# Row maxima of masked attention scores by another VectorE instruction, with the requests for the shifts and the value products placed elsewhere

## The chip, the cores and the metric

The kernel runs on one core of a Trainium2 chip. The metric is device time in microseconds of one execution; a median over several executions is compared. The engines are TensorE (PE; its weight loads are shown as PEld), VectorE (DVE), ScalarE (ACT), GpSimd (POOL) and SyncE (SP, which here issues DMAs).

## What is computed

One layer: the rows of x (8 batches of 512 rows, 128 wide) are normalised, and the result goes through causal attention with 16 heads of 8 dimensions and through a mixture of 8 experts with top-2 routing beside one shared expert. Everything is added to x.

```python
def attn(x, W1, b1, Wp, bp):              # B, S, E = 8, 512, 128; H = 16 heads, d = 8
    h = x @ W1 + b1                       # q, k, v for each head
    w = einsum('bhqd,bhkd->bhqk', q, k) / sqrt(d)
    w = softmax(w * mask - (1.0 - mask) * 1e6, axis=-1)   # mask: lower triangle
    a = einsum('bhqk,bhkd->bhqd', w, v)
    return a @ Wp + bp

def ffn(x):                               # 4096 rows; hidden width 352
    shared = (silu(x @ gate.T) * (x @ up.T)) @ down.T
    probs = softmax(x @ gate_w.T); topw, topi = top_k(probs, 2)
    routed = sum over the two chosen experts of topw / sum(topw) * expert(x)
    return shared + routed

xn = layernorm(x)
out = x + attn(xn) + ffn(xn)
```

Everything is float32.

## The kernel before

**Groups, tiles and steps.** Attention goes by groups: a group n is four heads of one batch, so there are 8 x 4 = 32 groups. A group takes NTILES = 5 steps, one for each entry of TILES: two "wide" tiles, two "mixed" and one "half". Each holds 2 x 512 columns of scores for 128 keys a block. 32 x 5 = 160 steps make the main loop.

**What a step issues.** The order is written out by hand for PE, DVE, ACT and SP. A step does, in program order: on an odd group at i == 1 `fetch` (q and k of a later unit, on SP's queue); `weigh`, which computes transposed scores in PSUM (`fill`, tile scT, L339) and their exponential on ScalarE (pT, L465), with the triangle cut either by extra products (L324) or afterwards by POOL (L472); the pending writes of expert results (`to_place`); `look` for the tile nine steps ahead (AHEAD); `extra`, one piece of the expert layer (`chunk`: products gu, L651, tanh on ScalarE, L656, and two VectorE operations, L657 and L659), which also issues `load_weights` (L602, SP's queue, 576 KB an expert) and `load_slots` on POOL; one slice of the routing, until it is done; `side`, which runs what has fallen due and the down products (y, L682); and the value products that are waiting (`late`).

**Why row maxima are needed.** The exponential must have its row maximum subtracted. In the transposed scores a row's maximum would lie along partitions, so the maximum is worked out beforehand from scores that aren't transposed (`look`, `maxima`, `peak_scores`: products sc, L383) and put into q as two additional rows (a high and a low part) against rows of ones in k. `shift_parts` makes the two parts on VectorE at the group's last tile, `shift` turns them on TensorE (mT_ps, L439) and copies them (mT, L443) a step later, and `put_shift` sends them with two DMAs from SP into rows of qs (L449) a step after that. scT of the group then reads these rows.

**Row maxima before.** tops and diag hold maxima of 2 x 2 x 4 blocks of rows. For i = 0 and 2 (MASKED_TILES) the tile holds only the diagonal blocks, eight products of 128 columns. The mask comes in one of two ways: while the routing runs, by four products with the mask (mask_half, L324); afterwards `prepare` has ScalarE write the mask into the PSUM tile a step ahead (L371), and the products add to it. One reduction over 1024 columns gives diag (L417). For i = 1 and 3 the blocks in front of the diagonal of rows 3 and 1 are computed (384 and 128 columns for each of two heads) and reduced (L421, L422); for i = 4 those of row 2 for four heads (256 columns each; L412). tops starts at -3e38; row_max is the larger of tops and diag (L427).

**PSUM and SBUF.** The sc tile has one buffer of two banks (m_ps), scT one of two banks (w_ps), the value sums one bank (av_ps), and three banks (mi_ps) go round for all else, gu and y among them. pT comes from a pool of four buffers (pr).

**Value products.** `attend` multiplies pT with v_ext (av, L489), four heads side by side in four columns of the array. It is called twice in a group: behind step 1 for the two wide tiles (it runs in step 2), and behind step 4 for the mixed and half ones (it runs in step 0 of the next group).

**When the routing is over**, `some_routing` closes the pools that it used and opens those of the routed experts (later_pools).

Of the kernel before, what the change touches and what calls it, by code (L numbers as in the profile page):

```python
# [67 lines left out]
def attn_moe_kernel(  # L68
# [72 lines left out]
    def constant_rows(t, rows):  # L141
# [4 lines left out]
                fills[:rows].unsqueeze(1).to_broadcast([rows, NU * HP * NC, P]),  # L146
            )

    mask_q = const.tile([P, P], BF16, name="mask_q")
    nc.gpsimd.memset(mask_q, 0.0)  # L150
    nc.gpsimd.affine_select(
        out=mask_q, in_=mask_q, pattern=[[-1, P]], compare_op=ALU.is_ge, fill=MASKED,
        base=0, channel_multiplier=1,
    )
    eye_2 = const.tile([P, 2, P], BF16, name="eye_2")
    mask_q2 = const.tile([P, 2, P], BF16, name="mask_q2")
    mask_k2 = const.tile([P, 2, P], BF16, name="mask_k2")
    for m, sign, compare, fill in (
        (mask_q2, 1, ALU.is_ge, MASKED), (mask_k2, -1, ALU.is_ge, MASKED),
        (eye_2, 1, ALU.not_equal, 1.0),  # L160
    ):
# [29 lines left out]


    tops = const.tile([P, 2, 2, NC], F32, name="tops")
    nc.vector.memset(tops, LEAST)
    diag = const.tile([P, 2, 2, NC], F32, name="diag")

    xnT = const.tile([E, NT * P], F32, name="xnT")

# [162 lines left out]

    MASKED_TILES = (0, 2)
    ahead = []

    def prepare(n, i):

        ps = m_ps.tile([P, 2, S], F32, name="sc")
        if i in MASKED_TILES:  # L370
            nc.scalar.copy(  # L371
                ps.rearrange("p t (b k) -> p (t b) k", k=P),
                mask_q.unsqueeze(1).to_broadcast([P, 2 * NC, P]),
            )
        ahead.append(ps)

    def peak_scores(n, i):
        ready_ = bool(ahead)
        ps = ahead.pop() if ready_ else m_ps.tile([P, 2, S], F32, name="sc")

        def part(at_, jj, c, key, count, start):
            q, k = rows_of(n, jj, QK + 1 if n else QK)
            nc.tensor.matmul(  # L383
                ps[:, jj % 2, ts(at_, P) if count == 1 else ds(at_ * P, count * P)],
                lhsT=q[:, ts(c, P)], rhs=k[:, key * P : (key + count) * P],
                start=start, stop=True, skip_group_check=True,
            )

        j = i // 2 * 2
        if i == 4:  # L390
            blocks = [(0, 0, 2, 0, 2, True), (2, 2, 2, 0, 2, False)]
        elif i in MASKED_TILES:
            blocks = [(c, j, c, c, 1, not ready_ and c == 0) for c in range(NC)]
        else:
            blocks = [(0, j, 3, 0, 3, True), (3, j, 1, 0, 1, False)]
        for at_, jj, *rest in blocks:
            for t in range(2):
                part(at_, jj + t, *rest)
        if i in MASKED_TILES and not ready_:
            for k in range(2):  # L400
                for t in range(2):
                    mask_half(
                        ps[:, t].rearrange("p (b k) -> p b k", k=P), t, k,
                        mask_q2[ts(t, SIDE), k].unsqueeze(1).to_broadcast([SIDE, NC, P]),
                    )
        return ps

    def maxima(n, i):

        ps = peak_scores(n, i)  # L410
        if i == 4:
            nc.vector.tensor_reduce(  # L412
                tops[:, :, :, 2],
                ps.rearrange("p t (u k) -> p t u k", u=2), AX.X, ALU.max,
            )
        elif i in MASKED_TILES:
            nc.vector.tensor_reduce(  # L417
                diag[:, :, i // 2, :], ps.rearrange("p t (b k) -> p t b k", k=P), AX.X, ALU.max
            )
        else:  # L420
            nc.vector.tensor_reduce(tops[:, :, i // 2, 3], ps[:, :, : 3 * P], AX.X, ALU.max)  # L421
            nc.vector.tensor_reduce(tops[:, :, i // 2, 1], ps[:, :, 3 * P :], AX.X, ALU.max)  # L422

    def shift_parts(n):

        top = at.tile([P, 2, 2 * NC], F32, name="row_max")
        nc.vector.tensor_tensor(  # L427
            top.rearrange("p t (i c) -> p t i c", c=NC), tops, diag, ALU.max
        )
        parts = at.tile([P, 2, 2, 2 * NC], F32R, name="m_parts")  # L430
        hi, lo = parts[:, :, 0], parts[:, :, 1]
        nc.vector.tensor_scalar_mul(hi, top, -1.0)
        nc.vector.scalar_tensor_tensor(lo, top, -1.0, hi.bitcast(F32), ALU.mult, ALU.subtract)
        return parts

    def shift(n, parts):

        ps = misc([32, P], "mT_ps")
        nc.tensor.transpose(  # L439
            ps, parts.rearrange("p t r m -> p (t r m)").bitcast(F32), ident  # L440
        )
        mT = at.tile([32, P], F32R, name="mT")
        nc.vector.tensor_copy(mT, ps)  # L443
        return partial(put_shift, n, mT)

    def put_shift(n, mT):
        for t in range(2):
# [5 lines left out]
                mT[ts(t, 16)].bitcast(F32),  # L453
            )

    masked = []

    def on_pool():
        return tc.issue_after(masked[-1]) if masked else nullcontext()
# [1 line left out]
    def weigh(n, kind, j, by_pool, spare):  # L461

        ps = fill(n, kind, j, by_pool, spare)
        pT = pr.tile([P, 2, S], F32, name="pT")
        nc.scalar.activation(pT, ps, AF.Exp, scale=D**-0.5)  # L465
        if by_pool:
            if kind == "half":
                diagonals = [pT.rearrange("p t (u k) -> p (t u) k", u=2)[:, :, :P]]
            else:
                diagonals = [pT[:, :, :P]] + ([pT[:, :, 3 * P :]] if kind == "mixed" else [])  # L470
            for d in diagonals:
                m = nc.gpsimd.affine_select(  # L472
                    out=d, in_=d, pattern=[[0, d.shape[1]], [1, P]], compare_op=ALU.is_ge,
                    fill=0.0, base=0, channel_multiplier=-1,
                )
                masked.append(m.ins)
        return pT

    def attend(n, tiles, av):

        b, g = divmod(n, NG)

        def add(jj, c, weights):
            at_ = HH * (g % 2) + 4 * (g // 2) + jj
            nc.tensor.matmul(  # L489
                av[32 * jj : 32 * jj + 32, c * P :], lhsT=v_ext[b % NV][:, c, at_, :],  # L490
                rhs=weights, start=(c == 0 and g % 2 == 0), stop=(c == NC - 1 and g % 2 == 1),
                skip_group_check=True,
            )

        heads = [(j + t, pT[:, t]) for _, j, pT in reversed(tiles) for t in range(2)]
        if len(tiles) > 2:
            attend(n, tiles[:-1], av)
            attend(n, tiles[-1:], av)
            return
        kind = tiles[0][0]  # L500
        if kind == "wide":
            for jj, w in heads:
                add(jj, 0, w)
        elif kind == "mixed":
            for jj, w in heads:
                add(jj, 1, w[:, : 3 * P])
            for jj, w in heads:
                add(jj, 3, w[:, 3 * P :])
        else:
            for t, w in heads:  # L510
                for u in range(2):
                    add(2 * u + t, 2, w[:, ts(u, 2 * P)])
# [74 lines left out]
    stream += [("routed", j) for j in range(NB // MB)]  # L587
    stream += [("shared", j) for j in shared[FIRST:]]
    weights, held, turned, scales = {}, {}, {}, {}
    later_pools = {}  # L590

    def load_weights(k, c):

# [559 lines left out]
    def some_routing():  # L1153
        if not done_routing and next(routing, "end") == "end":
# [3 lines left out]
            later_pools["inp"] = pool("inp", 6)  # L1158
            later_pools["turned"] = pool("turned", 3)
            later_pools["scales"] = pool("scales", 4)  # L1160

    measure(0, NC)
    scale(0, 1)
# [45 lines left out]
    routed = -2  # L1209
    alone = set(range(3, 21, 2)) | {12, 16, 20}  # L1210
    for t in range(AHEAD):
        parts_then = look(t)
        extra()
        parts_then()
        if t - AHEAD >= routed:
            some_routing()
        side(t - AHEAD, 2)
        behind(t - AHEAD)
    for n in range(B * NG):
        b, g = divmod(n, NG)  # L1220
        waiting = []
        for i, (kind, j) in enumerate(TILES):
            step = n * NTILES + i
            if i == 1 and n % 2 == 1 and (n + 3) // 2 < 2 * B:
# [3 lines left out]
            waiting.append((kind, j, weigh(n, kind, j, by_pool, spare)))  # L1228
            while to_place:
                to_place.pop(0)()  # L1230
            parts_then = look(step + AHEAD) if step + AHEAD < total_steps else lambda: None
            if step not in alone:
                extra()
            parts_then()
            if done_routing and step + AHEAD + 1 < total_steps:
                prepare(*divmod(step + AHEAD + 1, NTILES))
            if step >= routed:
                some_routing()
            side(step, 2)
# [5 lines left out]
                evacuate(n, av, halves[0])  # L1245
            if i == 1 and g % 2 == 0:
                av = av_ps.tile([P, S], F32, name="av")
            if i in (1, 4) or (i == 3 and n == B * NG - 1):
                late = [partial(attend, n, waiting, av)]
                waiting = []  # L1250
            if len(placed) == NB:
# [89 lines left out]
```

## Time and profile before

| | |
|---|---|
| median of 3 executions | 564.23 us (562.38 to 564.98) |
| the profiled execution | 565.0 us, of which the span from first to last instruction is 562.8 us |
| granted TensorE clock, mean | 0.992 |

| group of instructions | count | mean of one |
|---|---|---|
| L383 sc, 128 / 256 / 384 columns | 620 / 124 / 124 | 259 / 296 / 380 ns |
| L417 diag, 1024 columns | 64 | 1221 ns |
| L421, L422, L412 tops, 768 / 256 / 1024 columns | 64 / 64 / 32 | 950 / 412 / 1220 ns |
| L371 ScalarE writes the mask | 50 | 1020 ns |
| L324 products with the mask into sc | 56 | 382 ns |
| L465 exponential | 156 | 1025 ns |
| L657, L659 VectorE for gu | 156, 156 | 416, 423 ns |
| L427 row_max | 32 | 166 ns |
| L602 expert weights, 576 KB | 40 | |
| L449 shifts into qs, 8 KB | 64 | |

A line of groups names line, engine, operation, tiles and shapes, count, then busy time and mean of one, then idle time before it and what ended that. A line of the timeline gives start, length, engine, line, operation and, in brackets, the idle time before it. Durations of products are pipelined: two in a row overlap, so elapsed time is read from start to start. SPq is SP's issue of DMAs. The profile tells 14 tiles with the mask by products and 50 with the mask by ScalarE, and the routing's last piece on VectorE is at 141 us.

### The profile page before, as it was taken

To read this page: it belongs to the slowest core of one execution; us is meant where nothing else is said; L and a number is where in the kernel's file an instruction comes from. 1 tells how busy PE (TensorE), PEld (TensorE's weight loads), DVE (VectorE), ACT (ScalarE), POOL (GpSimd) and SP (SyncE) were. 2 spreads that over 40 slices of the span, in tenths; PEclk is the share of its full clock that TensorE was granted. 3 is DMA by queue.
4 is the path that set the end of the run, shared out by engine and by line. 5 is a ranking of instruction groups with operands and counts; after the bars stand their busy time and mean duration, and the time that the engine had idled before them with its cause. 6 is when DMAs were issued, how large, how long until landed. Compare 5 with 4: busy or idle time off the path is not lost.

```text
span 562.8 us, 12501 instructions
## 1 busy us (share of the span) xinstructions
PE 530.4 (94%) x4495; PEld 381.8 (68%) x4495; DVE 435.0 (77%) x1057; ACT 354.6 (63%) x567; POOL 261.8 (47%) x442
## 2 busy tenths in 40 slices
PE   4899988889999999999999999999999999989994
PEld 3676655557675777777776777667776777768762
DVE  5878998999877877777786887777787877877731
ACT  4453444463566866777677776677677767766553
POOL 8630020001342656666556656656555755543730
PEclk9999998899999999999999999999999999999999
DMA  7651362616228495685829584775928596750694
GB/s 217 146 75 19 77 116 58 96 59 122 65 64 142 131 154 147 118 204 115 156 72 160 176 137 124 129 168 134 175 84 152 154 155 185 147 135 4 103 255 95
DMA packets 34114, 70.72 MB, mean 126 GB/s; under 512 B 7028, under 2 KB 9336, under 8 KB 34054
## 3 DMA queue, kind: packets, MB, share of 16 engines
q1 hardware_dynamic: 26278, 56.47, 45.7%
q0 software_dynamic: 6912, 13.20, 12.3%
q8 instruction: 36, 0.59, 0.5%
q10 hardware_dynamic: 864, 0.27, 0.2%
q14 instruction: 24, 0.20, 0.2%
HBM read 52.38 MB, written 17.33 MB: 124 GB/s over the span
## 4 chain that ended last, share of the span: by engine, by line
PE 76%; DVE 18%; DMA 2%; ACT 2%; issue 2%; SPq 0%; DVEq 0%; ACTq 0%
PE gu L651 25%; PE av L489 12%; PE y L682 11%; PE scT L339 9%; PE sc L383 9%; DVE diag L417 3%; PE qk_ps L264 3%; DVE there L1065 2%; DMA qs<-mT 2%; DVE tops L421 2%; DVE h L659 1%; DVE th L657 1%; PE s_ps L627 1%; PE p_ps L577 1%; PE ot L540 1%
## 5 line engine op out<-in xcount | busy, mean ns | idle before, releaser
L465 ACT ACTIVATE pT<-scT 128x1024 f32<-128x1024 f32 x156 | 159.9, 1025 | 66.3 <-PE scT L339 28.3
L472 POOL TENSOR_SCALAR_AFFINE_SELECT pT<-pT 128x256 f32<-128x256 f32 (+1 forms) x174 | 73.7, 437 | 186.5 <-ACT pT L465 182.8
L651 PE MATMUL gu<-sT,w 128*128 128x256 f32 (+1 forms) x480 | 122.5, 382 | 0.3 <-DVE h L659 0.3
L417 DVE TENSOR_REDUCE diag<-sc 128x8 f32<-128x1024 f32 x64 | 78.2, 1221 | 45.1 <-PE sc L383 32.4
L656 ACT ACTIVATE th<-gu 128x256 f32<-128x256 f32 x156 | 59.8, 383 | 65.5 <-PE gu L651 61.0
L383 PE MATMUL sc<-ks,qs 33*128 33x128 f32 (+3 forms) x896 | 81.9, 282 | 9.9 <-DVE tops L422 4.2
L651 PEld LDWEIGHTS gu<-sT,w 128*128 128x128 f32 x480 | 76.6, 189 | 17.2 <-DVE h L659 0.5
L489 PE MATMUL av<-pT,v_ext 128*32 128x512 f32 (+3 forms) x1024 | 82.9, 441 | 1.8 <-ACT pT L465 1.3
L657 DVE SCALAR_TENSOR_TENSOR th<-th,gu 128x256 f32<-128x256 f32 x156 | 64.9, 416 | 23.2 <-ACT th L656 19.0
L339 PE MATMUL scT<-qs,ks 35*128 35x512 f32 (+3 forms) x498 | 78.6, 372 | 3.5 <-DMA qs<-mT 2.3
L666 POOL DMA_INDIRECT results<-o,goal x72 | 73.2, 1016 | 16.2 <-issue 16.2
L613 POOL DMA_INDIRECT s<-table,token x72 | 69.9, 971 | 21.0 <-issue 16.7
L339 PEld LDWEIGHTS scT<-qs,ks 35*128 35x128 f32 x498 | 39.6, 184 | 58.7 <-issue 24.9
L383 PEld LDWEIGHTS sc<-ks,qs 33*128 33x128 f32 (+1 forms) x896 | 66.9, 187 | 17.8 <-DVE diag L417 4.9
L659 DVE TENSOR_TENSOR h<-gu,th 128x256 f32<-128x256 f32 x156 | 66.0, 423 | 5.4
L421 DVE TENSOR_REDUCE tops<-sc 128x2 f32<-128x768 f32 x64 | 60.8, 950 | 1.8 <-PE scT L339 0.5
L682 PE MATMUL y<-w,h 128*128 128x128 f32 x432 | 60.0, 275 | 0.7 <-DVE parts L266 0.7
L682 PEld LDWEIGHTS y<-w,h 128*128 128x128 f32 x432 | 57.2, 191 | 4.6 <-DVE parts L266 1.1
L371 ACT CAST sc<-mask_q 128x1024 f32<-128x1024 bf16 x50 | 51.0, 1020 | 6.1 <-DVE tops L422 4.5
L651 PE MATMUL gu<-xnT,ws_sb 128*128 128x256 f32 x192 | 54.1, 408 | 0.0
L489 PEld LDWEIGHTS av<-pT,v_ext 128*32 128x32 f32 x1024 | 25.4, 109 | 24.0 <-issue 14.4
L412 DVE TENSOR_REDUCE tops<-sc 128x4 f32<-128x1024 f32 x32 | 39.0, 1220 | 2.3 <-PE sc L383 2.0
(209 smaller groups left out, 577.5 us busy)
## 6 DMA issues: line engine op xcount, KB each, us to landing
w<-in_w_exp_dram SPq DMA_DIRECT2D x40, 576.0 KB
ks<-dk SPq DMA_DIRECT2D x60, 128.0 KB
dq<-parts SPq DMA_DIRECT2D x16, 256.0 KB
dk<-parts SPq DMA_DIRECT2D x16, 256.0 KB
qs<-dq SPq DMA_DIRECT2D x64, 64.0 KB
x_sb<-results POOLq DMA_DIRECT2D x16, 256.0 KB
qs<-dq SPq DMA_DIRECT2D x30, 128.0 KB
table<-rows SPq DMA_DIRECT2D x4, 520.0 KB
```

The source lines that it names most:

```text
L339: nc.tensor.matmul(out_, lhsT=k[:, ts(i, P)], rhs=q[:, i * P :], start=first, stop=True, skip_group_check=True,)
L383: nc.tensor.matmul(ps[:, jj % 2, ts(at_, P) if count == 1 else ds(at_ * P, count * P)], lhsT=q[:, ts(c, P)], rhs=k[:, key * P : (key + cou ...
L417: nc.vector.tensor_reduce(diag[:, :, i // 2, :], ps.rearrange("p t (b k) -> p t b k", k=P), AX.X, ALU.max)
L421: nc.vector.tensor_reduce(tops[:, :, i // 2, 3], ps[:, :, : 3 * P], AX.X, ALU.max)
L465: nc.scalar.activation(pT, ps, AF.Exp, scale=D**-0.5)
L472: m = nc.gpsimd.affine_select(out=d, in_=d, pattern=[[0, d.shape[1]], [1, P]], compare_op=ALU.is_ge, fill=0.0, base=0, channel_multiplier=-1,)
L489: nc.tensor.matmul(av[32 * jj : 32 * jj + 32, c * P :], lhsT=v_ext[b % NV][:, c, at_, :], rhs=weights, start=(c == 0 and g % 2 == 0), stop ...
L651: nc.tensor.matmul(gu[:, i, part], lhsT=w[c][:, ds(i * FP + f * P, P)], rhs=sT[:, part], start=True, stop=True,)
L657: nc.vector.scalar_tensor_tensor(th, th, 1.0, gu[:, 0], ALU.add, ALU.mult)
L659: nc.vector.tensor_tensor(h[own_, f], gu[own_, 1], th[own_], ALU.mult)
L666: d = nc.gpsimd.indirect_dma_start(results, bass.IndirectOffsetOnAxis(ap=goal[:, at_ : at_ + 1], axis=0), o, None, bounds_check=PLACES - 1 ...
L682: nc.tensor.matmul(y, lhsT=h[:, f, ts(c, P)], rhs=w[c % len(w)][:, ds(2 * FP + f * P, P)], start=(f == 0), stop=(f == NF - 1),)
```

## The change

Four things change.

- `peak_scores` computes, for i = 0 and 2, row block 3 whole, with its diagonal block (512 columns, two heads: two products instead of eight). For i = 1 and 3 it computes row block 2 (384) and row block 0 (128), both with their diagonal; for i = 4 row block 1 (256) for four heads.
- `maxima` issues, for each head and row block, one `tensor_tensor_reduce` on VectorE: it adds to the scores a part of a new constant `until` (128 x 512 bfloat16, 0 up to the diagonal of the last block, -1e30 behind it), writes the sum back to PSUM, and writes the row maximum to tops. A group has 16 of them. prepare, diag, row_max, mask_q and mask_q2 are gone.
- `shift` puts put_shift into a list, `puts`, that is emptied right behind `to_place`, in front of `look` and `extra`, instead of running it in the next step's `side`.
- Once the routing is over, all but the last group call `attend` once, behind step 4, for all five tiles; `attend` then goes kind by kind (wide, mixed, half). For this pT gets three more buffers (prob_later): of seven tiles in a row four come from the old pool and three from the new.

```diff
-    nc.vector.memset(tops, LEAST)
-    diag = const.tile([P, 2, 2, NC], F32, name="diag")
+    until = const.tile([P, S], BF16, name="until")
+    nc.gpsimd.memset(until, 0.0)
+    nc.gpsimd.affine_select(
+        out=until, in_=until, pattern=[[-1, S]], compare_op=ALU.is_ge, fill=MASKED,
+        base=S - P, channel_multiplier=1,
+    )
...
+    def peak_scores(n, i):
         ps = m_ps.tile([P, 2, S], F32, name="sc")
...
         if i == 4:
-            blocks = [(0, 0, 2, 0, 2, True), (2, 2, 2, 0, 2, False)]
-        elif i in MASKED_TILES:
-            blocks = [(c, j, c, c, 1, not ready_ and c == 0) for c in range(NC)]
+            blocks = [(0, 0, 1), (2, 2, 1)]
+        elif i % 2 == 0:
+            blocks = [(0, j, 3)]
         else:
-            blocks = [(0, j, 3, 0, 3, True), (3, j, 1, 0, 1, False)]
+            blocks = [(0, j, 2), (3, j, 0)]
+        for at_, jj, c in blocks:
             for t in range(2):
+                q, k = rows_of(n, jj + t, QK + 1 if n else QK)
+                nc.tensor.matmul(
+                    ps[:, t, ds(at_ * P, (c + 1) * P)], lhsT=q[:, ts(c, P)],
+                    rhs=k[:, : (c + 1) * P], start=(at_ == 0), stop=True,
+                    skip_group_check=True,
+                )
+        return ps, blocks
 
     def maxima(n, i):
 
-        ps = peak_scores(n, i)
...
+        ps, blocks = peak_scores(n, i)
+        for at_, jj, c in blocks:
+            for t in range(2):
+                cols = slice(at_ * P, (at_ + c + 1) * P)
+                nc.vector.tensor_tensor_reduce(
+                    ps[:, t, cols], ps[:, t, cols], until[:, S - (c + 1) * P :], 1.0, LEAST,
+                    ALU.add, ALU.max, tops[:, t, jj // 2, c : c + 1],
+                )
 
     def shift_parts(n):
 
-        top = at.tile([P, 2, 2 * NC], F32, name="row_max")
-        nc.vector.tensor_tensor(
-            top.rearrange("p t (i c) -> p t i c", c=NC), tops, diag, ALU.max
-        )
+        top = tops.rearrange("p t i c -> p t (i c)")
...
-        return partial(put_shift, n, mT)
+        puts.append(partial(put_shift, n, mT))
...
-        pT = pr.tile([P, 2, S], F32, name="pT")
+        here = pr
+        if "prob" in later_pools:
+            here = (pr, later_pools["prob"])[len(taken) % 7 >= 4]
+            taken.append(here)
+        pT = here.tile([P, 2, S], F32, name="pT")
...
+        kinds = [tile_[0] for tile_ in tiles]
+        if len(set(kinds)) > 1:
+            for kind in dict.fromkeys(kinds):
+                attend(n, [tile_ for tile_ in tiles if tile_[0] == kind], av)
+            return
...
+            later_pools["prob"] = pool("prob_later", 3)
...
+        whole = "prob" in later_pools and n < B * NG - 1
...
             while to_place:
                 to_place.pop(0)()
+            while puts:
+                puts.pop(0)()
             parts_then = look(step + AHEAD) if step + AHEAD < total_steps else lambda: None
             if step not in alone:
                 extra()
             parts_then()
-            if done_routing and step + AHEAD + 1 < total_steps:
-                prepare(*divmod(step + AHEAD + 1, NTILES))
...
-            if i in (1, 4) or (i == 3 and n == B * NG - 1):
+            if i == 4 or (i == 1 and not whole) or (i == 3 and n == B * NG - 1):
                 late = [partial(attend, n, waiting, av)]
```

More of the change, by code (lines that the diff above doesn't have):

```diff
@@ L147, in constant_rows @@
             )
[L149 to L153, printed above, removed]
-    )
     eye_2 = const.tile([P, 2, P], BF16, name="eye_2")
-    mask_q2 = const.tile([P, 2, P], BF16, name="mask_q2")
     mask_k2 = const.tile([P, 2, P], BF16, name="mask_k2")
     for m, sign, compare, fill in (
-        (mask_q2, 1, ALU.is_ge, MASKED), (mask_k2, -1, ALU.is_ge, MASKED),
+        (mask_k2, -1, ALU.is_ge, MASKED),
         (eye_2, 1, ALU.not_equal, 1.0),
@@ L357, in fill @@
         return ps
-    MASKED_TILES = (0, 2)
-    ahead = []
-    def prepare(n, i):
+    def peak_scores(n, i):
         ps = m_ps.tile([P, 2, S], F32, name="sc")
[L370 to L387, printed above, removed]
@@ L389, in peak_scores @@
         j = i // 2 * 2
         if i == 4:
-            blocks = [(0, 0, 2, 0, 2, True), (2, 2, 2, 0, 2, False)]
-        elif i in MASKED_TILES:
-            blocks = [(c, j, c, c, 1, not ready_ and c == 0) for c in range(NC)]
-        else:
-            blocks = [(0, j, 3, 0, 3, True), (3, j, 1, 0, 1, False)]
-        for at_, jj, *rest in blocks:
+            blocks = [(0, 0, 1), (2, 2, 1)]
+        elif i % 2 == 0:
+            blocks = [(0, j, 3)]
+        else:
+            blocks = [(0, j, 2), (3, j, 0)]
@@ L397, in peak_scores @@
+        for at_, jj, c in blocks:
             for t in range(2):
[L398 to L406, printed above, removed]
-    def maxima(n, i):
-        ps = peak_scores(n, i)
[L411 to L422, printed above, removed]
+                q, k = rows_of(n, jj + t, QK + 1 if n else QK)
[4 more added lines that the diff above has]
+                )
@@ L427, in shift_parts @@
-        nc.vector.tensor_tensor(
-            top.rearrange("p t (i c) -> p t i c", c=NC), tops, diag, ALU.max
-        )
+        top = tops.rearrange("p t i c -> p t (i c)")
         parts = at.tile([P, 2, 2, 2 * NC], F32R, name="m_parts")
@@ L443, in shift @@
         nc.vector.tensor_copy(mT, ps)
-        return partial(put_shift, n, mT)
+        puts.append(partial(put_shift, n, mT))
+    puts = []
     def put_shift(n, mT):
@@ L454, in put_shift @@
             )
-    masked = []
+    masked, taken = [], []
+    later_pools = {}
     def on_pool():
@@ L493, in add @@
             )
+        kinds = [tile_[0] for tile_ in tiles]
[3 more added lines that the diff above has]
+            return
         heads = [(j + t, pT[:, t]) for _, j, pT in reversed(tiles) for t in range(2)]
[L496 to L499, printed above, removed]
         kind = tiles[0][0]
@@ L589, in attn_moe_kernel @@
     weights, held, turned, scales = {}, {}, {}, {}
-    later_pools = {}
     def load_weights(k, c):
@@ L1230, in attn_moe_kernel @@
                 to_place.pop(0)()
+            while puts:
+                puts.pop(0)()
             parts_then = look(step + AHEAD) if step + AHEAD < total_steps else lambda: None
```

## The prediction

> **What bounds the kernel now.** I read the page's busy times first, then busy time by stage, then the chain of waits of each stage, and last the timeline of one group of heads.
>
> ```profile
> PE 530.4 (94%) x4495; PEld 381.8 (68%) x4495; DVE 435.0 (77%) x1057; ACT 354.6 (63%) x567; POOL 261.8 (47%) x442
> ```
>
> The average hides two regimes. By stage (length, then busy time of PE, PEld, DVE, ACT, POOL):
>
> ```profile
> 27.00:60.00 33.00, 31.86 (x222) 22.04 (x219) 27.13 (x57) 14.47 (x31) 6.87 (x22) 1.00 0.30 42
> 60.00:145.00 85.00, 75.64 (x743) 48.96 (x741) 80.21 (x235) 41.92 (x57) 6.13 (x12) 0.96 0.44 89
> 145.00:530.00 385.00, 379.85 (x3189) 281.60 (x3187) 297.00 (x658) 269.84 (x435) 219.68 (x319) 1.00 0.62 132
> ```
>
> From 60 to 145 us, while the routing is worked out, VectorE is busy 80.2 of 85 us. From 145 to 530 us TensorE is busy 379.9 of 385 and VectorE has 23% to spare. The pieces of the chain of waits in these windows, added up by engine, say the same: VectorE 64.3 and TensorE 14.1 of the 85 us; TensorE 23.2 and VectorE 9.2 of the 33 us before; and in the long stage it is TensorE nearly throughout:
>
> ```profile
> by line: PE gu L651 31.5%; PE av L489 15.4%; PE y L682 13.6%; PE scT L339 12.7%; PE sc L383 10.5%; PE qk_ps L264 2.7%; PE s_ps L627 1.8%; DVE diag L417 1.5%; PE p_ps L577 1.4%; DMA qs<-mT 1.4%; PE ot L540 1.4%; PE v_ps L284 0.9%; DVE parts
> ```
>
> So a microsecond taken from TensorE counts after 145 us, and one added to VectorE counts before it. The diagonal reductions fall 5, 9 and 49 into the three stages, all reductions' tiles 11, 24 and 122: 2.2, 4.8 and 24.4 groups of five.
>
> **Row maxima, TensorE's side.** Of five score tiles of a group two (i = 0 and 2) hold only diagonal blocks: eight products of 128 columns. They become two of 512; the other three tiles keep their widths. Elapsed time is read from the start of scT to the start of gu (the durations are pipelined and overlap):
>
> ```profile
> 333.56 0.50 PE L339 MATMUL scT<-qs,ks 35*128 35x512 f32 x2
> 333.89 0.56 PE L383 MATMUL sc<-ks,qs 33*128 33x128 f32 x8
> 334.38 1.13 PE L651 MATMUL gu<-sT,w 128*128 128x256 f32 x4
> ...
> 345.12 0.50 PE L339 MATMUL scT<-qs,ks 35*128 35x512 f32 x2
> 345.45 0.40 PE L383 MATMUL sc<-ks,qs 33*128 33x256 f32 x4
> 345.78 1.13 PE L651 MATMUL gu<-sT,w 128*128 128x256 f32 x4
> ```
>
> Two of 512 take 0.33 us here (345.12 to 345.45), the eight of 128 took 0.49 (333.89 to 334.38), and 0.55 behind a mixed tile (340.00 to 340.55). That saves 0.16 and 0.22; I take 0.41 us for the two tiles of a group, 24.4 x 0.41 = 10.0 us in the long stage. Before the routing is over the same tiles also carry a mask added by four products:
>
> ```profile
> 73.74 0.64 PE L383 MATMUL sc<-ks,qs 33*128 33x128 f32 x8
> 74.22 0.61 PE L324 MATMUL sc<-mask_q,eye 64*128 64x512 bf16 x4
> 74.76 0.70 PE L651 MATMUL gu<-xnT,ws_sb 128*128 128x256 f32 x2
> ```
>
> 1.02 us become 0.34, so 0.68 for each of 14 tiles. Only what lies on TensorE's part of the chain counts: 5 x 0.68 x 23.2/33 = 2.4 us in the first stage, 9 x 0.68 x 14.1/85 = 1.0 in the second. ScalarE loses its 50 mask copies (51.0 us), which I price at nothing: TensorE was busy beside them already.
>
> **Row maxima, VectorE's side.** The elements stay 5120 a group (5 x 1024 before, 4 x (512 + 384 + 128 + 256) after). The count changes: seven reductions and one row_max become 16 instructions that add the mask and reduce.
>
> ```profile
> L417 DVE TENSOR_REDUCE diag<-sc 128x8 f32<-128x1024 f32 x64 | 78.2, 1221 | 45.1 <-PE sc L383 32.4
> ...
> 337.05 0.96 DVE L421 TENSOR_REDUCE tops<-sc 128x2 f32<-128x768 f32 x1
> 337.92 0.42 DVE L422 TENSOR_REDUCE tops<-sc 128x2 f32<-128x256 f32 x1
> ```
>
> From 1221 ns at 1024 elements and 412 at 256 (L422), an element costs 1.053 ns. L422 starts 0.87 us behind L421, whose 768 elements cost 0.81: an independent instruction in a row has a fixed cost f of about 0.065 us start to start. The new instruction isn't in this trace. Its f has two bounds: 0.065, if writing the maximum out is free, and 0.215, if that write is a second, dependent instruction (row_max to the next tiny one, 333.22 to 333.42, is 0.20, so the main's 0.065 plus some 0.15 for a tiny one alone). I take 0.135, twice the independent cost: a second instruction in the same pipe, with no semaphore between, is nearest to that row. Per group then 16 x 0.135 - 7 x 0.065 - 0.20 (row_max) = +1.5 us; the bounds give +0.4 and +2.8. On VectorE's part of the chain: 4.8 x 1.5 x 64.3/85 = +5.4 us from 60 to 145, and 2.2 x 1.5 x 9.2/33 = +0.9 before.
>
> [...]
>
> **Whether VectorE takes over after 145 us.** In the group from 333.56 to 348.94 the four steps without the long burst (to 345.12) take 11.56 us on TensorE; less 1.0 for the wide value products that move and 0.41 saved, 10.15. VectorE's work there: 12 of the new instructions over 4096 elements, 4.31 + 12 f; four times 0.82 for th and h; some 1.4 of the rest (11.9 us a group at 77%, less reductions, th, h and row_max, by four fifths). With f = 0.135 that is 10.6: VectorE falls 0.45 us behind. TensorE may run ahead, as the next sc waits only for the reductions of the last, about 1.1 us (th, h and the rest) before VectorE is free. So the lag is covered, and the step with the burst (some 4.9 us of TensorE) makes it good. I add 2.5 us for uneven steps, about as much as TensorE's idle time in this stage has besides the DMA wait (5.2 - 2.3). In that step the products queued behind the burst, scT and sc of the next step, wait for it; VectorE starves, which costs nothing while TensorE is the bound.
>
> **The burst.** The eight wide products take 1.0 us for 512 columns, the other 24 take 1.43 for 768; by proportion the columns cost 1.68 ns each (0.43/256), so each burst has some 0.14 us of entry and joining saves at most that: 0 to 3.4 us over 24 groups. I take 1. Seven weight tiles instead of four keep ScalarE from waiting for a free one until the burst has read them.
>
> **The shifts.** put_shift leaves its place behind extra(), and with it SP's queue order against load_weights (one or two issues of 576 KB, against its own two of 8 KB). Where both fall into one step, it hurts:
>
> ```profile
> 496.23 1.52 SPq L602 DMA_DIRECT2D w<-in_w_exp_dram  x2
> 497.85 1.41 SPq L449 DMA_DIRECT2D qs<-mT  x2
> ...
> 503.26 0.58 PE L339 MATMUL scT<-qs,ks 35*128 35x512 f32 x2 [2.26 <-DMA qs<-mT]
> ```
>
> mT was ready at 494.3, so both rows could go some 3 us earlier and in front of 1.2 MB: that idle 2.26 us goes; the exponential before it had ended at 500.8, so TensorE's own work is next. A second wait, 0.95 us at 545.9 behind a shift that was asked for as soon as mT existed, has no weights in front; I count half, so 2.8 us. Behind the wait for mT SP now holds load_weights, for products two blocks later: covered by about six steps; if it weren't, each late load would stop gu. fetch still goes first. The constant masks on POOL change by under 1 us before 14 us, ahead of the first sc at 26.1.
>
> **Sum.** -2.4 + 0.9 - 1.0 + 5.4 - 10.0 + 2.5 - 1.0 - 2.8 = -8.4 us. The profiled execution took 565.0 us (span 562.8), so 556.6; the median shown, 564.2, lies 0.8 below it, so **556 us**.
>
> **Rivals.**
> 1. *The maximum's write-out is dear* (f = 0.215; for it, small dependent instructions; against it, the 0.065 row). Place: VectorE between the reductions. 60 to 145 us: 4.8 x 2.8 x 64.3/85 = +10.2; before, +1.7. After: 4.31 + 12 x 0.215 + 3.3 + 1.4 = 11.6, a lag of 1.45, 0.35 over the cover, x 24.4 = +8.5. Sum -2.4 + 1.7 - 1.0 + 10.2 - 10.0 + 2.5 + 8.5 - 1.0 - 2.8 = +5.7: **570 us**, slower. It decides from f = 0.18 up, where the interpolated sum changes sign.
> 2. *The write-out is free* (f = 0.065): +1.4 and +0.2 for the two early stages, 1.0 of uneven steps, joining 3.0: -2.4 + 0.2 - 1.0 + 1.4 - 10.0 + 1.0 - 3.0 - 2.8 = -16.6: **548 us**.
> 3. *TensorE's saving doesn't show*, because the pace after 145 us moves to VectorE and ScalarE latencies as soon as TensorE gives way (for it, ScalarE's 4.5 us behind VectorE's tops; against it, TensorE's 99%): the sum without the 10.0 is +1.6, **566 us**, no change.
>
> **Chances.** Forecast 0.43, free 0.15, dear 0.27, no saving 0.15. What a measurement can tell is about 0.5%, 2.8 us. Faster: the first two. Same: most of the third and a little of the dear case near its sign change, 0.14. Slower: the rest, 0.28. The forecast's own range is 551 to 562; to hold 8 in 10 it reaches down to the free case, 548, and up past the dear one, 575.
>
> **What would show it.** sc x2 of 512 in about 0.33 us, and no mask copies on ScalarE; the new instruction 0.59 to 0.75 us for 512 elements and under 0.70 start to start; VectorE busy near 87% from 145 to 530 us with TensorE still at 98% or more; the stage from 60 to 145 us about 4 us longer; no wait on qs<-mT near 500 us. The prediction is wrong if scT or sc wait for the reductions in most steps, if 512 elements take over 0.75 us start to start, or if the joined burst leaves ScalarE or TensorE waiting for weight tiles.

## The result, and the profile after

The changed kernel takes 593.4 us (median of 4 runs, 591.26 to 594.99) beside 563.31 us for the kernel before (4 runs, 562.31 to 564.98): a ratio of 1.05 with a 95% interval of 1.045 to 1.0551. The forecast was 556 us with a range of 548 to 575. Here and below a ratio comes from all fast executions and can differ a little from the quotient of the medians; two slow executions of the sixteen plain reductions (560.21 and 691.75 us) and one of the kernel that keeps grouped reductions until the routing is over (569.39 us) are in their medians but not in their ratios. The profiled execution took 594.99 us with a span of 593.1; before it was 565.0 with 562.8.

The page of the kernel after: busy time by engine, the chain that ended last by engine, and the two groups into which each new instruction falls.

```profile
PE 533.2 (90%) x4055; PEld 364.3 (61%) x4055; DVE 498.0 (84%) x1824; ACT 309.9 (52%) x517; POOL 261.7 (44%) x439
...
PE 48%; DVE 41%; issue 4%; DMA 3%; ACT 2%; POOL 1%; SPq 0%; DVEq 0%; ACTq 0%; POOLq 0%
...
L386 DVE CUSTOM_DVE_ANT_0 sc<-sc,until 128x384 f32<-128x384 f32 (+3 forms) x512 | 254.1, 496 | 40.2 <-PE sc L373 26.6
...
L386 DVE DVE_READ_ACCUMULATOR2_ANT tops<- 128x1 f32 x512 | 72.0, 141 | 0.0
```

TensorE has 440 instructions fewer, but VectorE has 767 more and 63 us more to do. On the page of before the chain's shares were 76% for TensorE and 18% for VectorE; now they are 48% and 41%. The line of before:

```profile
PE 76%; DVE 18%; DMA 2%; ACT 2%; issue 2%; SPq 0%; DVEq 0%; ACTq 0%
```

The group lines of after tell what the new instruction is: 512 times a main instruction, and 512 times a second one of 141 ns that reads the accumulated maximum out into one column of tops.

By stage (length, busy time of PE, PEld, DVE, ACT, POOL with their instructions, granted clock, DMA share, GB/s), after:

```profile
27.00:60.00 33.00, 28.84 (x173) 19.82 (x173) 29.55 (x103) 13.93 (x30) 7.17 (x23) 0.98 0.30 43
60.00:145.00 85.00, 68.84 (x569) 41.08 (x567) 79.34 (x304) 36.41 (x49) 4.32 (x8) 0.85 0.35 76
145.00:530.00 385.00, 364.06 (x2751) 255.34 (x2744) 336.16 (x1222) 218.63 (x371) 209.14 (x305) 1.00 0.60 133
```

In the long stage VectorE is busy 87% of the time, as the prediction said, but TensorE is no longer full: 364.1 of 385 us, not the 98% that the prediction asked for. What it waits for is in the list of waits (engine, line, releaser: us in total, times, longest), after:

```profile
PEld sc L373 <- DVE tops L386: 45.1, 57, 2.4
...
PE sc L373 <- DVE tops L386: 30.4, 46, 2.2
```

Before, these were its main waits for reductions when it came to sc, 7.3 us together. Now it is 30.4.

```profile
PE sc L383 <- DVE tops L422: 4.2, 6, 1.3
...
PE sc L383 <- DVE diag L417: 3.1, 4, 1.4
```

The new instruction by itself, in VectorE's timeline after (start and duration in us; in brackets the idle time before and what ended it):

```profile
354.83 0.70 DVE L386 CUSTOM_DVE_ANT_0 sc<-sc,until 128x512 f32<-128x512 f32 x1 [0.86 <-PE sc L373]
355.45 0.14 DVE L386 DVE_READ_ACCUMULATOR2_ANT tops<- 128x1 f32 x1
355.62 0.70 DVE L386 CUSTOM_DVE_ANT_0 sc<-sc,until 128x512 f32<-128x512 f32 x1
```

From start to start a maximum over 512 elements takes 0.79 us (354.83 to 355.62). For 384, 256 and 128 elements the same reading gives 0.66, 0.525 and 0.39 us, so an element costs 1.042 ns and the rest, the fixed cost f of the prediction, is **0.257 us** between two in a row, at all four widths. It has two parts: the read starts 0.62 us behind the main instruction, 0.087 more than 512 elements cost, and the next main instruction starts 0.17 us behind the read.

The last maximum of a tile costs less, because the operation behind it (th, mostly) starts together with the read. Four maxima over 256 elements and the th behind them, first and last rows:

```profile
350.89 0.42 DVE L386 CUSTOM_DVE_ANT_0 sc<-sc,until 128x256 f32<-128x256 f32 x1
...
352.80 0.14 DVE L386 DVE_READ_ACCUMULATOR2_ANT tops<- 128x1 f32 x1
352.80 0.42 DVE L628 SCALAR_TENSOR_TENSOR th<-th,gu 128x256 f32<-128x256 f32 x1
```

That is 1.91 us to th for 1024 elements of 1.042 ns, so 0.21 for each of the four. By the same reading a tile of two maxima over 512 takes 1.40 us (median). A group has two such tiles and three of four maxima: 8.53 us, an f of **0.20 us** on average. The seven reductions and row_max of before take 5.99 (5.33 for the elements, 7 x 0.065 and 0.20), so a group costs VectorE 2.5 us more, where the prediction had 1.5.

TensorE's side, in its timeline after:

```profile
354.06 0.50 PE L336 MATMUL scT<-qs,ks 35*128 35x512 f32 x2
354.39 0.40 PE L373 MATMUL sc<-ks,qs 33*128 33x512 f32 x2
354.72 1.13 PE L622 MATMUL gu<-sT,w 128*128 128x256 f32 x4
```

Two products of 512 columns take 0.33 us (354.39 to 354.72): the saving on this side is there, as large as predicted.

Where the time came from can be read from the start of each step's exponential. How much later it starts than before:

| step | 0 | 10 | 20 | 30 | 60 | 100 | 140 | 159 |
|---|---|---|---|---|---|---|---|---|
| later by, us | 0.4 | 4.1 | 10.2 | 13.6 | 17.2 | 21.0 | 24.3 | 30.3 |

Some 13 us are lost by step 28, while the routing is worked out, where the prediction had +2.9 for both early stages together. After that each step loses a little more, where the prediction had a gain of some 11 us.

### The profile page after: what moved, and what is told of

Same layout as the page of the kernel before. It is cut to its first block, busy times and chain, and to the rows that moved or that the text cites. A ratio compares the mean times of both kernels' runs of the same rounds, so it can differ in the third digit from the quotient of the medians.

```text
span 593.1 us, 12354 instructions
## 1 busy us (share of the span) xinstructions
PE 533.2 (90%) x4055; PEld 364.3 (61%) x4055; DVE 498.0 (84%) x1824; ACT 309.9 (52%) x517; POOL 261.7 (44%) x439
## 4 chain that ended last, share of the span: by engine, by line
PE 48%; DVE 41%; issue 4%; DMA 3%; ACT 2%; POOL 1%; SPq 0%; DVEq 0%; ACTq 0%; POOLq 0%
DVE sc L386 22%; PE gu L622 13%; PE av L460 11%; PE y L653 6%; PE sc L373 6%; PE scT L336 5%; DVE tops L386 3%; DVE th L628 3%; DVE h L630 3%; PE qk_ps L261 2%; DVE there L1036 2%; PE p_ps L549 1%; DVE mT L407 1%; DMA w<-in_w_exp_dram 1%; DMA ks<-dk 1%
## 5 line engine op out<-in xcount | busy, mean ns | idle before, releaser
L386 DVE CUSTOM_DVE_ANT_0 sc<-sc,until 128x384 f32<-128x384 f32 (+3 forms) x512 | 254.1, 496 | 40.2 <-PE sc L373 26.6
L373 PE MATMUL sc<-ks,qs 33*128 33x384 f32 (+5 forms) x512 | 76.2, 353 | 32.8 <-DVE tops L386 30.4
L584 POOL DMA_INDIRECT s<-table,token x72 | 69.9, 971 | 20.9 <-issue 15.0
L373 PEld LDWEIGHTS sc<-ks,qs 33*128 33x128 f32 (+1 forms) x512 | 42.2, 187 | 50.7 <-DVE tops L386 45.1
L386 DVE DVE_READ_ACCUMULATOR2_ANT tops<- 128x1 f32 x512 | 72.0, 141 | 0.0
L622 PE MATMUL gu<-xnT,ws_sb 128*128 128x256 f32 x192 | 55.4, 415 | 0.7 <-DVE h L630 0.7
L460 PEld LDWEIGHTS av<-pT,v_ext 128*32 128x32 f32 x1024 | 29.3, 114 | 38.5 <-issue 32.2
L660 ACT ACTIVATE o<-y,scale 128x128 f32<-128x128 f32 x72 | 26.4, 367 | 28.9 <-PE y L653 20.8
L622 PEld LDWEIGHTS gu<-xnT,ws_sb 128*128 128x128 f32 x192 | 34.0, 196 | 11.5 <-issue 4.2
```

What stands on the lines that cost most here:

```text
L373: nc.tensor.matmul(ps[:, t, ds(at_ * P, (c + 1) * P)], lhsT=q[:, ts(c, P)], rhs=k[:, : (c + 1) * P], start=(at_ == 0), stop=True, skip_gro ...
L386: nc.vector.tensor_tensor_reduce(ps[:, t, cols], ps[:, t, cols], until[:, S - (c + 1) * P :], 1.0, LEAST, ALU.add, ALU.max, tops[:, t, jj ...
L460: nc.tensor.matmul(av[32 * jj : 32 * jj + 32, c * P :], lhsT=v_ext[b % NV][:, c, at_, :], rhs=weights, start=(c == 0 and g % 2 == 0), stop ...
L584: nc.gpsimd.indirect_dma_start(s[:, c], None, table, bass.IndirectOffsetOnAxis(ap=token[:, at_ : at_ + 1], axis=0),)
L622: nc.tensor.matmul(gu[:, i, part], lhsT=w[c][:, ds(i * FP + f * P, P)], rhs=sT[:, part], start=True, stop=True,)
```

## The experiments

Four theories. **A**: the fixed cost of the new instruction, 16 times a group. **B**: the joined burst holds TensorE so long that another engine starves. **C**: the early shifts hold up the weight loads in SP's queue. **D**: it is the number of VectorE instructions, of whatever kind. Later P stands for the forecast's gain from the early shifts, and L for a burst that costs because VectorE already lags. Ratios are to the kernel before on the same chip; its medians were 558.9, 564.16 and 561.18 us on the three chips, so times are not compared across them.

### The row maxima alone

```diff
--- after
-        puts.append(partial(put_shift, n, mT))
+        return partial(put_shift, n, mT)
...
-        whole = "prob" in later_pools and n < B * NG - 1
+        whole = False
```

> The kernel before with only the row maxima changed (no shifts moved, no joined burst). Theory A, the new VectorE instruction's fixed cost (0.257 us start to start in the trace of after) makes the whole loss: 593.4 us plus the 1 to 4 us that burst and shifts were worth, 594 to 598 us. Theory B, the joined burst starves VectorE and ScalarE and makes a good part of it: 575 to 585 us. Theory C, the moved shifts hold up SP's weight loads: 585 to 590 us.

The seven weight tiles stay in this run. Measured: 579.92 us, ratio 1.0354 (1.0293 to 1.0415). That is most of the loss, but less than A wanted if the maxima were all of it. It lies in B's range, also when the ratio is put on 563.31 us (583 us): the maxima and something else both cost.

### Everything but the row maxima

```diff
--- before
-        return partial(put_shift, n, mT)
+        puts.append(partial(put_shift, n, mT))
...
+            here = (pr, later_pools["prob"])[len(taken) % 7 >= 4]
...
-            if i in (1, 4) or (i == 3 and n == B * NG - 1):
+            if i == 4 or (i == 1 and not whole) or (i == 3 and n == B * NG - 1):
```

> The kernel before with the shifts moved and the burst joined, its row maxima as they were. Theory A: 563.3 less 1 to 4 us, 559 to 562 us. Theory B: 572 to 582 us. Theory C: 566 to 570 us, and waits for weights at gu.

Measured: 566.41 us, ratio 1.0124 (1.0055 to 1.0193). A's expectation missed, and so did B's 572 to 582 us: the shifts and the burst together cost something by themselves, where the prediction had a gain of 3.8 us. TensorE waits only 0.7 us for weights in this run, so C explains little of the 7.5 us (566.41 - 558.9), though the time alone would fit its 566 to 570; the two parts had to be run alone.

### Sixteen plain reductions

```diff
--- after
-                nc.vector.tensor_tensor_reduce(
-                    ps[:, t, cols], ps[:, t, cols], until[:, S - (c + 1) * P :], 1.0, LEAST,
-                    ALU.add, ALU.max, tops[:, t, jj // 2, c : c + 1],
+                nc.vector.tensor_reduce(
+                    tops[:, t, jj // 2, c : c + 1], ps[:, t, cols], AX.X, ALU.max
                 )
```

> The changed kernel with each of the 16 instructions replaced by a plain reduction of the same block; this leaves out the mask in the row maxima, so a row is shifted by the maximum over its whole diagonal block. Theory A (the price lies in the write-out of the maximum, a second instruction of 0.17 us): a fixed cost near 0.065 us a reduction, VectorE 16 x 0.19 = 3.1 us a group shorter, TensorE the bound again, 546 to 553 us. Rival D (the price lies in the count, any instruction on a block costs this much): 588 to 594 us. Theory B: 570 to 580 us.

Measured: 556.19 us, ratio 0.9943 (0.9903 to 0.9983). That is somewhat above A's range and far below those of D and B. The same count, blocks and order, and the loss is gone: D falls, and so does B as the main cause, since the joined burst is still in. VectorE's timeline shows the price of a plain reduction (four in a row: 384, 384, 128 and 128 elements):

```profile
349.62 1.41 DVE L386 TENSOR_REDUCE tops<-sc 128x1 f32<-128x384 f32 x4
350.95 0.41 DVE L627 SCALAR_TENSOR_TENSOR th<-th,gu 128x256 f32<-128x256 f32 x1
```

1.33 us for 1024 elements of 1.042 ns, 1.067, leaves 0.066 us for each of the four. That is the prediction's 0.065 from L421 and L422: it holds for reductions. By the same reading, up to the next operation, the new instruction costs 0.21, three times as much, and between two in a row four times.

### Seven reductions over both heads

```diff
--- after
         ps, blocks = peak_scores(n, i)
+        if i == 4:
+            nc.vector.tensor_reduce(
+                tops[:, :, :, 1], ps.rearrange("p t (u k) -> p t u k", u=2), AX.X, ALU.max
+            )
+            return
         for at_, jj, c in blocks:
-            for t in range(2):
...
+            cols = slice(at_ * P, (at_ + c + 1) * P)
+            nc.vector.tensor_reduce(tops[:, :, jj // 2, c], ps[:, :, cols], AX.X, ALU.max)
```

> As the last, with seven reductions a group, each over both heads (mask in the row maxima left out). Theory A: VectorE's load is that of the kernel before less row_max; TensorE's saving of some 10 us in the long stage, 2 to 3 us before it and 3 to 4 us of burst and shifts show: 545 to 551 us, within 3 us of the 16 reductions. Rival D: about 16 x 0.25 - 7 x 0.25 = 2.2 us a group below the 16 reductions, 540 to 560 us with those at 590. Theory B: 570 to 580 us.

Measured: 548.87 us, ratio 0.9817 (0.9749 to 0.9884). With the reductions at their old price, the change's TensorE side does bring time. A's "within 3 us of the 16 reductions" missed: seven are some 7 us faster than sixteen, so the count costs something too, only far less than D had it.

### The early shifts alone

```diff
--- before
-        return partial(put_shift, n, mT)
+        puts.append(partial(put_shift, n, mT))
...
                 to_place.pop(0)()
+            while puts:
+                puts.pop(0)()
             parts_then = look(step + AHEAD) if step + AHEAD < total_steps else lambda: None
```

> The kernel before with only the shifts asked for earlier. Theory P (the early request takes away the DMA wait of 2.3 us and costs nothing): 2 to 3 us below before, ratio 0.995. Rival C (SP waits for mT in front of the weight loads, and gu then for weights): ratio 1.008 to 1.015, which would be the 7 us that shifts and burst cost together on before's row maxima.

Measured: 564.62 us, ratio 1.0006 (0.9975 to 1.0037). Neither expectation: no gain, and nothing lost to the weights. The wait near 500 us is gone in its trace, and no other wait of TensorE for qs is left. Its SP issues there:

```profile
495.58 0.35 SPq L604 DMA_DIRECT2D w<-in_w_exp_dram  x1
496.03 1.38 SPq L451 DMA_DIRECT2D qs<-mT  x2
498.84 0.34 SPq L604 DMA_DIRECT2D w<-in_w_exp_dram  x1
```

The rows now go between the two weight issues, which the program makes in two steps in a row, and not in front of both, as the prediction had it. The interval excludes a gain of 2.8 us (0.5%); what took the place of the wait that went is not settled.

### The joined burst alone

```diff
--- before
+            here = (pr, later_pools["prob"])[len(taken) % 7 >= 4]
...
-        if len(tiles) > 2:
-            attend(n, tiles[:-1], av)
-            attend(n, tiles[-1:], av)
-            return
...
-            if i in (1, 4) or (i == 3 and n == B * NG - 1):
+            if i == 4 or (i == 1 and not whole) or (i == 3 and n == B * NG - 1):
```

> The kernel before with only the joined burst and its seven weight tiles. Theory L (the burst crowds VectorE's and ScalarE's work into four steps, and costs where these are near their limit): ratio 1.008 to 1.02 here, as ScalarE still writes the masks. Rival (burst neutral, the cost was the shifts'): 0.994 to 1.002.

Measured: 567.78 us, ratio 1.0064 (1.0031 to 1.0097). A cost, below L's figure and above its rival's. Here VectorE doesn't lag; the list of waits of this run from 145 to 530 us names another engine:

```profile
PEld sc L383 <- ACT sc L371: 10.0, 14, 1.3
...
PE sc L383 <- ACT sc L371: 7.0, 14, 1.0
```

L371 is ScalarE's copy of the mask into the next sc tile, which the kernel before still makes. Without the joined burst (the early shifts alone, same chip) TensorE waits 0.6 us for it. With it TensorE waits 14 times, 7.0 us, and its busy time in this stage is 375.6 us where it was 380.8. So the burst delays what TensorE needs next from an engine beside it; here that is the mask copy.

### The change without its joined burst

```diff
--- after
-        whole = "prob" in later_pools and n < B * NG - 1
+        whole = False
```

> The changed kernel with its value products in two bursts again; row maxima and shifts as changed. Theory L: the loss after the routing goes away, 577 to 582 us where the row maxima alone gave 580 (ratio 1.03 to 1.04). Rival (the new instruction's price alone makes the loss in both stages): 588 to 594 us, ratio 1.05.

Measured: 585.65 us, ratio 1.0376 (1.0329 to 1.0423). The ratio is the one that L gave, and the rival's 1.05 is excluded: beside the whole change's 1.05 (and 1.0477 below), the burst costs about 1% in it. But L's 577 to 582 us was missed, and no gain behind the routing came back: the loss doesn't go away with the burst (its exponentials start 15.5 us later than before's at step 28 and 20.9 us later at the end).

### Grouped reductions without the joined burst

The edit of the seven reductions and that of the last run together.

> Seven plain reductions a group on the changed products (the mask in the row maxima left out: a row is shifted by the maximum over its whole diagonal block), shifts early, value products in two bursts. Theory L: 0 to 8 us below the same kernel with the joined burst (ratio to before 0.968 to 0.982), less than on the slower row maxima, since VectorE has room here. Rival (the burst costs by itself, whatever VectorE's load): 7 us or more below it, 0.970 or less.

Measured: 553.48 us, ratio 0.9807 (0.9768 to 0.9846), against 0.9817 with the burst joined. Where VectorE has slack and no mask copy is left, joining neither costs nor brings anything that these runs can tell.

### Grouped until the routing is over, the new instruction behind it

```diff
--- after, with whole = False
         ps, blocks = peak_scores(n, i)
+        if not done_routing:
+            if i == 4:
+                nc.vector.tensor_reduce(
+                    tops[:, :, :, 1], ps.rearrange("p t (u k) -> p t u k", u=2), AX.X, ALU.max
+                )
+                return
+            for at_, jj, c in blocks:
+                cols = slice(at_ * P, (at_ + c + 1) * P)
+                nc.vector.tensor_reduce(tops[:, :, jj // 2, c], ps[:, :, cols], AX.X, ALU.max)
+            return
         for at_, jj, c in blocks:
             for t in range(2):
```

> Two bursts, shifts early; the seven plain reductions until the routing is over (there the mask in the row maxima is left out), the 16 new instructions behind it. Theory A by stages (the price counts where VectorE is the bound, and behind the routing two bursts leave room for it): the first stages gain 2 to 5 us on before, the long stage stays at before's pace: 558 to 563 us where before is 564 (ratio 0.99 to 1.0). Rival (the price counts in every stage alike): the long stage has 24.4 of 31.4 groups, so some 78% of the loss of 21 us stays: 576 to 580 us, ratio 1.02 to 1.03.

Measured: 560.74 us, ratio 0.9986 (0.9951 to 1.002). The ratio is in A's range and the rival's is excluded. But "before's pace" in the long stage isn't free: the same kernel with plain reductions throughout has 0.9807, so even with two bursts the new instruction uses up what TensorE saves there.

### The same with the joined burst, and the change once more

The first is the last kernel with `whole` as the change has it; the second is the changed kernel.

> The last with the joined burst. Theory L (the burst costs where VectorE is near its limit): 6 to 12 us over the last, ratio to before 1.003 to 1.015. Rival (burst neutral): as the last within 3 us.

> The changed kernel once more, beside these on one chip: ratio 1.045 to 1.055. Over the last, all theories: the price of the new instruction until the routing is over, 15 to 20 us.

Measured: 570.31 us, ratio 1.0163 (1.0109 to 1.0217), and 588.42 us, ratio 1.0477 (1.0429 to 1.0525). L's 6 to 12 us for the joined burst came, at a ratio just above its 1.015, and so did the 15 to 20 us. On one chip, then: the kernel that is grouped until the routing is over, with two bursts, beside the kernel before, -0.4 us; joining the bursts, +9.6 (570.31 - 560.74); the new instruction in place of grouped reductions while the routing is worked out, +18.1 (588.42 - 570.31).

The waits from the whole execution, first without the joined burst, then with it:

```profile
PEld sc L373 <- DVE tops L396: 16.0, 31, 1.1
...
PE sc L373 <- DVE tops L396: 6.4, 12, 0.8
```

```profile
PEld sc L373 <- DVE tops L396: 28.3, 52, 1.2
...
PE sc L373 <- DVE tops L396: 14.2, 31, 0.9
```

The timeline of a group with the joined burst (all engines; lines of others left out):

```profile
349.91 2.36 PE L470 MATMUL av<-pT,v_ext 128*32 128x512 f32 x32
...
352.54 0.39 PE L373 MATMUL sc<-ks,qs 33*128 33x512 f32 x2
...
352.99 0.70 DVE L396 CUSTOM_DVE_ANT_0 sc<-sc,until 128x512 f32<-128x512 f32 x1 [1.30 <-PE sc L373]
...
354.40 0.14 DVE L396 DVE_READ_ACCUMULATOR2_ANT tops<- 128x1 f32 x1
...
354.60 0.50 PE L373 MATMUL sc<-ks,qs 33*128 33x384 f32 x4
...
357.34 0.14 DVE L396 DVE_READ_ACCUMULATOR2_ANT tops<- 128x1 f32 x1
...
357.53 0.50 PE L373 MATMUL sc<-ks,qs 33*128 33x512 f32 x2
...
360.51 0.50 PE L373 MATMUL sc<-ks,qs 33*128 33x384 f32 x4 [0.31 <-DVE tops L396]
...
363.48 0.50 PE L373 MATMUL sc<-ks,qs 33*128 33x256 f32 x4 [0.77 <-DVE tops L396]
```

TensorE goes into the burst of 32 products at 349.91 and makes no sc until 352.54; VectorE runs dry and sits idle for 1.30 us. Over the next four steps VectorE falls behind. Its maxima of the first two are read out by 354.54 and 357.48, just in front of the sc that needs their place (354.60 and 357.53); for the next two TensorE waits, 0.31 and then 0.77 us. The next burst starts at 365.65. VectorE starves in the fifth step and comes to set the pace in the others, so the idle stretch is lost. With two shorter bursts (the list of waits above) TensorE waits 6.4 us for maxima in place of 14.2.

## Why the prediction was wrong

**The cost of the new instruction: the first step that failed.** The prediction took f = 0.135 us, "twice the independent cost", between bounds of 0.065 and 0.215. It is 0.257 between two in a row and 0.20 on average over a group. Both parts were too small: the main instruction has 0.087, not 0.065, and the read 0.17, not 0.15, where another maximum follows. The error was to choose the middle: the row nearest to the read, a tiny instruction behind the one it depends on, was the upper bound's own, and the read, 0.17 us here, belongs with it. So a group costs VectorE 2.5 us more, not 1.5.

**Where that cost lands: the second step, and the larger one.** Put f = 0.20 into the prediction's working, and the early stages have +9.2 and +1.6, the lag is 0.16 us over its cover (3.9 us over 24.4 groups), and the sum is nothing: 564 us, no change, where 593.4 was measured. (With 0.257 for all sixteen the working would give some 585, and the change without its joined burst took 585.65; but a group doesn't pay sixteen times 0.257, so that agreement is luck.) What failed is how the cost was weighed:

- While the routing is worked out, the prediction counted only VectorE's part of the chain, 64.3/85 and 9.2/33. The two kernels that differ in nothing but the new instruction there (34 tiles) differ by 18.1 us; VectorE's own time for these tiles differs by 18.4 (14 x 0.27 + 14 x 0.71 + 6 x 0.78, from the starts: 1.40, 1.91 and 1.91 us against 1.13, 1.20 and 1.13). All of it showed.
- Behind the routing the lag was to be covered by 1.1 us a step and made good in the burst's step. TensorE waits for maxima there all the same. Between the kernel that is grouped until the routing is over and the one that is grouped throughout, 0.9986 and 0.9807, lies the new instruction's price behind the routing: some 10 us (0.0179 x 561) with two bursts, on two chips. With the joined burst it is 1.0163 and 0.9817, some 19 us. In the group shown, the first two steps have some 0.05 us of cover left, not 1.1.

From 0.9807 the steps to the changed kernel are thus +1.8% for the new instruction behind the routing, +1.8% for the joined burst on top of it, and +3.1% for the new instruction in front: 1.0477.

The trace of after shows the operation as two instructions (512 and 512), which is the upper bound's reading; the trace of before has no such instruction. What pulled f below that bound was a row of another kind: the plain reduction's 0.065, which the sixteen plain reductions confirm (0.066) for themselves and for nothing else.

**The dear rival** had place and sign, and with f = 0.215 a cost per group close to the measured one (2.8 and 2.5 us). Its 570 us was too low because it took the same share of the chain and the same cover.

**The burst.** "VectorE starves, which costs nothing while TensorE is the bound" was the third step that failed. Joining does save what was read: the 32 products take 2.30 us (351.76 to 354.06), where 1.0 and 1.43 had been apart. But it cost 9.6 us where VectorE lags, and 0.64% in the kernel before, where it made mask copies late. The prediction had named scT and sc as queued behind the burst; it left out who feeds them. Seven weight tiles were enough: in the list of waits of after no exponential waits for value products to free one.

**TensorE's saving** was nearly right: 0.33 us for two products of 512, and with reductions at the old price (two bursts) the whole is 1.9% faster, 10.7 us (564.16 - 553.48), beside 10.0 + 2.4 + 1.0 predicted for TensorE; row_max is gone and the shifts are early in it too. So the third rival, that the saving doesn't show, holds only while VectorE sets the pace.

**The shifts.** The -2.8 us is a term that failed too; it wasn't measured in either place: alone the ratio is 1.0006, and the row maxima have 1.0376 with the early shifts and 1.0354 without them. In the changed kernel a wait of the same kind stands elsewhere (timeline after, SP's issues, then TensorE):

```profile
520.42 0.35 SPq L573 DMA_DIRECT2D w<-in_w_exp_dram  x1
520.87 1.38 SPq L415 DMA_DIRECT2D qs<-mT  x2
523.68 0.34 SPq L573 DMA_DIRECT2D w<-in_w_exp_dram  x1
...
527.53 0.59 PE L336 MATMUL scT<-qs,ks 35*128 35x512 f32 x2 [1.74 <-DMA qs<-mT]
```

The rows were asked for ahead of the second weight load but behind the first, which belongs to the step before. At the end it is as before: the last rows are on their way from 569.15 to 573.58 in the chain of waits, and TensorE stands for 1.9 us.

**The early stage** lost 13.0 us to step 28 where +2.9 was forecast. The regime was read rightly, VectorE's instructions there are on the path; but they cost 2.5 us a group, not 1.5, and all of that counted, not a share. TensorE ran at a lower granted clock there (from 60 to 145 us 0.85 against 0.96 before, and 0.83 against 0.96 in the two kernels that differ by 18.1 us); whether that clock has a part in the 18.1 us wasn't separated.

**The end** of the changed kernel loses 6.0 us more between steps 140 and 159 (24.3 to 30.3). Two steps hold nearly all of it: 2.4 us at step 156, behind that last wait, and 3.2 at step 141, where TensorE waits 0.47 us for expert weights and then runs on at a granted clock of 0.64 (530.0 to 534.7):

```profile
529.25 1.01 PE L622 MATMUL gu<-sT,w 128*128 128x128 f32 x6 [0.47 <-DMA w<-in_w_exp_dram]
530.06 1.50 PE L653 MATMUL y<-w,h 128*128 128x128 f32 x6
531.48 3.28 PE L460 MATMUL av<-pT,v_ext 128*32 128x512 f32 x32
```

Elsewhere in this trace the six y products take 0.83 us and the burst 2.36. The same kernel run once more loses only 2.5 us between these steps, so part of it belongs to the execution and not to the change.

**Open**: where the early shifts' gain went, and what sets the clock.

## The version that beats both

The seven reductions over both heads are 1.8% and 1.9% faster than the kernel before, with and without the joined burst; the two-burst form was run with the seven weight tiles, though the kernel before does with four. A row is shifted by the maximum over the whole diagonal block, not by that of its allowed keys. Softmax is unchanged by the shift; the price is range, since a row whose masked scores stand far above its allowed ones would see its exponentials underflow.

## What to carry to other kernels

The instruction that returns a maximum through an accumulator ran here as two, with 0.257 us of fixed cost between two in a row and 0.20 on average, beside 0.066 for a plain reduction: look for the second part before pricing one like it. Sixteen of these a group in place of seven reductions cost some 10 us behind the routing even with two bursts, though VectorE had 23% to spare there on average before: ask whether the engine has that much to spare in every step. Where a trace has no row for an operation, take the row of the same kind, a dependent pair here, and let the upper bound lie above it. Where an engine sets the pace already, count what is added to it whole (here 18.1 us showed of 18.4), and check a cover in the tightest step, not the average one. When a corrected term brings the sum to the measured time, check that the term is what a group really pays. Before products are joined into one burst, ask which engine makes the next step's input, and whether it can wait that long: the same joining cost 9.6 us where VectorE lagged, 3.6 us (567.78 - 564.16) where ScalarE was late with a mask copy, and nothing that could be measured where neither was.

## What the hardware showed that was not expected

From 60 to 145 us the granted clock of TensorE was 0.85 with the change, and 0.96 before. There TensorE waits 12.3 us for the maxima, beside 6.1 for reductions before (TensorE's timeline after):

```profile
90.57 0.80 PE L373 MATMUL sc<-ks,qs 33*128 33x256 f32 x4 [1.51 <-DVE tops L386]
91.30 2.07 PE L622 MATMUL gu<-xnT,ws_sb 128*128 128x256 f32 x4
```

Four products of 256 columns took 2.07 us, at a granted clock of 0.50 (91.3 to 93.4), where four of the same shape take 1.13 at 124.36, at a granted clock of 1.00 (124.3 to 125.4). The runs that share the new instruction in this stage had 0.80, 0.80 and 0.83 (the maxima alone, the change without its burst, the change once more), and those with plain or grouped reductions 0.92 to 0.96. The changed kernel has six waits of TensorE of over 1.2 us in this stage, the longest 2.2, where the kernel before has two, the longest 1.45: more and longer waits went with a lower clock. Which causes which wasn't tested.
